# A four-layer graph network on one core: where VectorE's scoring work is put beside a pair's last layer

## The chip, the cores and the metric

One core of one Trainium2 chip runs the kernel. The metric is the device time of one execution in microseconds (us): the median of several runs. One further execution was taken with the profiler; every line of the profile comes from that one.

## The reference, cut to what matters

The input x has 64 graphs of 256 nodes with 256 features; all share one sparse 256 x 256 matrix adj. Four layers follow each other. Layers 0, 1 and 3 are the same function with other weights:

```python
pre_u = einsum('bud,dk->buk', h, W1[:d]);  pre_v = einsum('bvd,dk->bvk', h, W1[d:])
hidden = relu(pre_u[:, :, None, :] + pre_v[:, None, :, :] + b1)
S = sigmoid(hidden @ W2 + b2)                      # one score for each pair of nodes
a = einsum('buv,bud->bvd', S * adj, h);  m = einsum('uv,bud->bvd', adj, h) * h
z = beta1 * h + beta2 * (a @ Wa + ba) + beta3 * (m @ Wm + bm)
```

Layer 2 is an attention layer over the same graphs: one logit per node, softmax of leaky_relu(f_i + f_j) + adj, then a product with the features and a residual.

## The kernel before, in words

Only the pairs of nodes that adj joins (the edges) are scored. They are laid out once as tiles of 128 edges. For one scored layer of two graphs, a tile's sums pre_u + pre_v come in one of two ways. A **made** tile is a matmul on TensorE: `ga<-pre,pick`, from rows that ScalarE copied to `pre`. A **fetched** tile is two indirect DMAs that GpSimd (POOL) issues: the rows of a table of pre_u are gathered (`fetched<-tableu`), then those of pre_v are added to them (`fetched<-tablev`). The tables are written to DRAM by SyncE's queue (`tableu<-pu`, `tablev<-pv`). Either way VectorE (DVE) then scores the tile with one instruction for each of two graphs (`junk<-ga` or `junk<-fetched`), which leaves one column in `raw`. Most scored layers have eight made and eight fetched tiles, two groups (own, two nodes' diagonal) and one tile `left` with what remains.

The columns are rated twice in a scored layer, by `rated_all` (L740): ScalarE's tanh `val<-raw`, an add, and four multiplies `rm<-gva,val` on VectorE. EARLY needs the first four fetched tiles (numbered 0 to 3 here), the first four made ones, the diagonal and `left`. LATE needs the other tiles and comes last, from `end()` (L808). After it TensorE can `spread` (L865) the scores into the matrix `sa` (`ps<-rm,gu`), which the layer's `finish` (L368) multiplies with the graphs. `early(st)` (L849) starts `sa` from EARLY's scores (`ps<-ro,guo`, `sa<-diag,val,ps`).

Four graphs are worked on at a time: the first pair (side "a") and the second pair (side "b"). The function `beside` (L911) writes one **unit** of the program: the scores of one pair's layer (heavy), and the other pair's dense work of the neighbouring layers (light), which is a generator. After each piece of light work it yields a step (p, f): so many made tiles and so many steps of the fetched ones are traced there. A plain number is p alone. Six units make a round, and there are 16 rounds. They are called here after the pair and the layer that is scored: A0, B0, A1, B1, A3, B3. The light work of B3 is the first pair's `after` of the last layer, then its next graphs' `before` of layer 0. The light work of A0 is the second pair's last layer and its next graphs' layer 0. `halfway` (L900) interleaves these two: four steps of `after`, two of `before`, the rest of `after`, the rest of `before`.

Three lists give the steps: `STEPS` (L45) for `finish`, the local list `beside` in `before` (L656) for the four blocks of pre_u and pre_v, and a step (99, 99) after them that takes all that is left.

The program is traced in this order, and a planner then orders each engine's instructions: trace order is the priority, but an instruction that its reckoning finds ready sooner may be issued first. `tc.issue_after(x)` keeps an instruction behind x on x's engine. The flag `placed` decides whether the scores use it:

- `stay` (L706) keeps made matmuls, scores of fetched tiles, `left`, the diagonal and `val` behind the last instruction traced on their engine, so they stand mid-unit where the steps put them. Without `placed` the planner may move them.
- In `got` (L783), with `placed`, the fifth fetched step needs four made tiles, rates EARLY, and `early(st)` is a step of its own. Without it, all made tiles are traced first, then `left` and EARLY in one step, and `early(st)` comes after the sixth fetched tile.

The third value that `stream` (L885) yields with a unit's light work is that unit's `placed`. For the unit beside the last layer it is `i > 0`, on both sides.

POOL's fetches are one chain in trace order: `fetch` (L814) puts each behind the one before. Each unit's first six are issued as soon as its tables' first half is traced.

Of the kernel before, what the change touches and what calls it, by code (L numbers as in the profile page):

```python
# [17 lines left out]
GNN = ("L0_gnn_", "L1_gnn_", "L3_gnn_")  # L18
LAST = GNN[2]
# [25 lines left out]
STEPS = {  # L45
    GNN[0]: [(1, 1), (1, 1), (0, 1), (1, 0), (0, 1), (2, 1)],
    GNN[1]: [0, 0, 0, (0, 1), (0, 1), 1],
    LAST: [1, (1, 1), 0, (1, 1), (0, 1), (2, 1)],
}

VEC = {}
# [11 lines left out]
def blk(c):  # L63
    return slice(c * P, (c + 1) * P)
# [37 lines left out]
def adj_seq_kernel(ctx: ExitStack, tc: tile.TileContext, a: dict, out: bass.AP):  # L102
# [44 lines left out]
    def sca(name):  # L147
        return scas[:, SCA[name] : SCA[name] + 1]
# [141 lines left out]
    def stages(pools):  # L290
# [7 lines left out]
        def psum():  # L298
            return ps.tile([P, 2, 256], FP, tag="ps", name="ps")

        def product(o, lhs, rhs):

            for m in range(2):
                for c in range(2):
                    mm(out=o[:, m, :], lhsT=lhs[:, c, blk(m)], rhs=rhs[:, c, :], start=c == 0, stop=c == 1)
# [7 lines left out]
        def hT_tile(st):  # L313
            return one.tile([P, 2, 2, N], FP, tag="hT" + st["side"], name="hT")

        def h_tile(st, g):
            return fm.tile([P, 2, D], FP, tag=f"h{g}" + st["side"], name=f"h{g}")

        def of_graph(x, b):
            return x[bass.ds(b, 1)].rearrange("b (p c d) -> (b p) c d", p=P, c=2)  # L320
# [32 lines left out]
        def kept(st, l):  # L353

            hb = one.tile([P, 2, 2, N], FP, tag="hb", name="hb")
            for i in range(2):
                if l == LAST:
                    for m in range(2):
                        vector.scalar_tensor_tensor(
                            hb[:, i, m, :], st["h"][i][:, m, :], sca(l + "beta1"), zbrow, ALU.mult, ALU.add  # L360
                        )
                else:
                    scalar.activation(
                        hb[:, i], st["hT"][:, i], AF.Identity, bias=zbias[l][:, i : i + 1], scale=sca(l + "beta1")
                    )
            return hb

        def finish(st, l):  # L368

            sa, mT = st["sa"], st["mT"]  # L370
            hb = kept(st, l)
            aT = one.tile([P, 2, 2, N], FP, tag="aT", name="aT")
            for g in range(2):
                t = psum()
                product(t, st["h"][g], sa[:, :, g, :])
                scalar.copy(aT[:, :, g, :], t)
                yield STEPS[l][g]
            if l == LAST:
                for g in range(2):
                    z = psum()  # L380
                    for m in range(2):
                        for j, (w, y) in enumerate(((wm[l], mT), (wa[l], aT))):
                            for c in range(2):
                                mm(out=z[:, m, :], lhsT=y[:, c, g, blk(m)], rhs=w[:, c, :],
                                   start=j == 0 and c == 0, stop=j == 1 and c == 1)
                        yield STEPS[l][2 + 2 * g + m]
                    o = h_tile(st, g)
                    vector.tensor_tensor(o, hb[:, g], z, ALU.add)
                    nc.sync.dma_start(
                        out=of_graph(out, st["b"] + g), in_=o  # L390
                    )
                return
            hT = hT_tile(st)
            for m in range(2):
                z = psum()
                for j, (w, y) in enumerate(((wm[l], mT), (wa[l], aT))):
                    for c in range(2):
                        mm(out=z, lhsT=w[:, c, blk(m)], rhs=y[:, c], start=j == 0 and c == 0, stop=j == 1 and c == 1)
                    if j == 0:
                        yield STEPS[l][2 + 2 * m]  # L400
                vector.tensor_tensor(hT[:, m], hb[:, m], z, ALU.add)
                yield STEPS[l][3 + 2 * m]
            st["hT"] = hT
            st["h"] = []

            def turn(g):
                t = psum()
                flip(t, hT[:, :, g, :])
                h = h_tile(st, g)
                if l == GNN[1]:  # L410

                    vector.tensor_tensor(h, t, bias2.unsqueeze(1).to_broadcast([P, 2, D]), ALU.add)
                else:
                    scalar.copy(h, t)
                st["h"].append(h)

            if l == GNN[1]:
                for g in range(2):
                    turn(g)
                    yield 0  # L420
            else:

                st["turn"] = turn
# [78 lines left out]
    def few(stack):  # L502
# [143 lines left out]
        def before(st, l):  # L646

            hT = st["hT"]
            pu = one.tile([P, 2, 2, D], FP, tag="pu" + st["side"], name="pu")
            pv = one.tile([P, 2, 2, D], FP, tag="pv" + st["side"], name="pv")  # L650
            pre = one.tile([P, len(FAST), 2 * D], FP, tag="pre" + st["side"], name="pre")
            order = [(m, g) for m in range(2) for g in range(2)]
            if l == LAST:
                order = [(m, g) for g in range(2) for m in range(2)]

            beside = {LAST: [0, (0, 1), (0, 1), (0, 1)], GNN[1]: [0] + [(0, 1)] * 3, GNN[0]: [(0, 1)] * 4}[l]  # L656
            beside = dict(zip(order, beside))
            st["tables"] = [
                tables.tile([N, 2 * D], FP, tag="table" + t + st["side"], name="table" + t) for t in "uv"
            ]  # L660

            st["pu"], st["pv"], st["pre"] = pu, pv, pre
            if l != GNN[1]:
                st["own"] = one.tile([P, 2, 2, D], FP, tag="own", name="own")
            t = one.tile([P, FIRST, 2, D], FP, tag="fetched" + st["side"], name="fetched")
            st["fetched"] = [t[:, f] for f in range(FIRST)]
            for m, g in order:
                if l == LAST and (m, g) == (1, 0):
                    st["flip"](1)
                t = psum()  # L670
                for c in range(2):
                    mm(out=t, lhsT=hT[:, c, g, blk(m)], rhs=w1[l][:, c], start=c == 0, stop=c == 1)
                scalar.copy(pu[:, m, g, :], t[:, 0, :])
                vector.tensor_tensor(pv[:, m, g, :], t[:, 1, :], b1row[l], ALU.add)
                if g == 1:
                    for rows, x in zip(st["tables"], (pu, pv)):
                        nc.sync.dma_start(out=rows[blk(m)], in_=flat(x)[:, m])
                    if m == 0:
                        st["fetches"] = list(FETCHES_MORE if more(st, l) else FETCHES)

                        if numbered:
                            fetch(st, AHEAD)
                if l != GNN[1]:
                    vector.tensor_tensor(st["own"][:, m, g, :], t[:, 0, :], pv[:, m, g, :], ALU.add)
                if g == 1:
                    if m == 0:
                        rows_u(st, 0, 2, 0, 0)
                    rows_v(st, 4 - 4 * m, 2, 0)
                    st["rows"] = scalar.last.ins
                yield beside[(m, g)]  # L690
                if l == GNN[1] and (m, g) == (0, 1):
                    st["turn"](0)
                    yield 0, 1
                    st["turn"](1)
                    yield 0
            yield REST_OF_IT

            yield from mixed(st, l, later if past else None, (0,) if more(st, l) else (0, 1))
# [186 lines left out]
        def stream(side, starts):  # L885

            sts = [{"b": b, "side": side} for b in starts]
            load(sts[0])
            short = [before(sts[0], GNN[0])]
            for i, st in enumerate(sts):  # L890
                yield short, (st, GNN[0]), i > 0
                yield [after(st, GNN[0]), before(st, GNN[1])], (st, GNN[1]), True
                yield [after(st, GNN[1]), attention(st), before(st, GNN[2])], (st, GNN[2]), False
                short = [after(st, GNN[2])]
                if i + 1 < len(sts):
                    load(sts[i + 1])
                    short = [halfway(after(st, GNN[2]), 4, before(sts[i + 1], GNN[0]), 2)]
            yield short, None, False
# [149 lines left out]
```

## Time and profile before

| what | us |
|---|---|
| median of 5 runs | 3474.66 |
| lowest and highest of them | 3470.12 and 3475.57 |
| the profiled execution | 3478.15 |
| its span, first to last instruction | 3476.4 |
| TensorE (PE) busy | 3365.6 |
| VectorE (DVE) busy | 2650.0 |
| POOL busy | 2412.7 |
| ScalarE (ACT) busy | 1556.3 |
| mean granted TensorE clock | 0.989 |

The profiled execution took 1.75 us more than its span, and 3.5 us more than the median. The page lists engines, DMA queues, the chain of work that ended last, and groups of instructions. Nearly all instructions have line 79, a helper, so groups are told apart by their tiles: `out<-in`. In a timeline row the columns are start, length, engine, line, operation, tiles, shapes, count, and in brackets the engine's idle time before it with what ended it.

### The profile page before, as it was taken

To read this page: it belongs to the slowest core of one execution; us is meant where nothing else is said; L and a number is where in the kernel's file an instruction comes from. 1 tells how busy PE (TensorE), PEld (TensorE's weight loads), DVE (VectorE), ACT (ScalarE), POOL (GpSimd) and SP (SyncE) were. 2 spreads that over 40 slices of the span, in tenths; PEclk is the share of its full clock that TensorE was granted. 3 is DMA by queue.
4 is the path that set the end of the run, shared out by engine and by line. 5 is a ranking of instruction groups with operands and counts; after the bars stand their busy time and mean duration, and the time that the engine had idled before them with its cause. 6 is when DMAs were issued, how large, how long until landed. Compare 5 with 4: busy or idle time off the path is not lost.

```text
span 3476.4 us, 48323 instructions
## 1 busy us (share of the span) xinstructions
PE 3365.6 (97%) x14200; PEld 2074.6 (60%) x14200; DVE 2650.0 (76%) x10523; ACT 1556.3 (45%) x2833; POOL 2412.7 (69%) x1882
## 2 busy tenths in 40 slices
PE   6999999999999999999999999999999999999998
PEld 3566565665656556565665656656565665656655
DVE  4777787877877777777777878777787777777776
ACT  2444444444444444544444444444444444444442
POOL 3667777677676767677677776776767776777774
PEclk7999999999999999999999999999999999999999
DMA  5788787887878878788787888778788887888875
GB/s 147 159 180 189 168 197 171 191 180 172 198 168 195 171 179 191 175 187 181 176 191 167 196 173 189 179 168 202 165 190 181 178 191 171 193 184 175 191 164 121
DMA packets 289070, 620.81 MB, mean 179 GB/s; under 512 B 39072, under 2 KB 56352, under 8 KB 288800
## 3 DMA queue, kind: packets, MB, share of 16 engines
q0 software_dynamic: 204800, 461.49, 66.4%
q1 hardware_dynamic: 82416, 154.96, 12.7%
q8 instruction: 115, 1.88, 0.2%
q10 hardware_dynamic: 1584, 1.20, 0.1%
q14 instruction: 155, 1.27, 0.1%
HBM read 500.06 MB, written 117.44 MB: 178 GB/s over the span
## 4 chain that ended last, share of the span: by engine, by line
PE 71%; POOL 9%; DMA 8%; issue 6%; DVE 4%; ACT 2%; ACTq 0%; POOLq 0%; DVEq 0%
PE ps L79 55%; PE ga L79 16%; POOL fetched L827 8%; DMA fetched<-tablev,ids_v 4%; DVE junk L79 2%; DMA fetched<-tableu,ids_u 2%; DMA tableu<-pu 1%; POOL left L827 1%; ACT pre L79 1%; DVE sa L79 1%; DVE rm L79 0%; ACT val L79 0%; ACT pu L79 0%; DVE own L79 0%; DVE pv L79 0%
## 5 line engine op out<-in xcount | busy, mean ns | idle before, releaser
L827 POOL DMA_INDIRECT fetched<-tablev,ids_v x832 | 1316.5, 1582 | 385.5 <-issue 254.4
L827 POOL DMA_INDIRECT fetched<-tableu,ids_u x832 | 839.9, 1010 | 553.3 <-DMA tableu<-pu 292.1
L79 DVE SCALAR_TENSOR_TENSOR junk<-fetched,L_gnn_w2row 128x256 f32<-128x256 f32 x1664 | 641.2, 420 | 209.0 <-DMA fetched<-tablev,ids_v 205.2
L79 PE MATMUL ga<-pre,pick 128*128 128x512 f32 x1408 | 726.6, 610 | 27.5 <-ACT pre L79 16.0
L79 PE MATMUL ps<-L_gnn_w,hT 128*128 128x512 f32 x1536 | 708.6, 599 | 5.5 <-DMA hT<-in_xT_dram 5.5
L79 DVE SCALAR_TENSOR_TENSOR junk<-ga,L_gnn_w2row 128x256 f32<-128x256 f32 x1408 | 536.1, 419 | 94.7 <-PE ga L79 85.4
L79 PEld LDWEIGHTS ps<-L_gnn_w,hT 128*128 128x128 f32 x1536 | 280.4, 191 | 324.3 <-issue 297.8
L79 ACT COPY pre<-pv 64x512 f32<-64x512 f32 x704 | 434.1, 617 | 62.6 <-DVE pv L79 49.7
L79 PE MATMUL ps<-sa,h 128*128 128x256 f32 x1536 | 367.6, 384 | 19.9 <-DVE sa L79 14.0
L79 PEld LDWEIGHTS ps<-sa,h 128*128 128x128 f32 x1536 | 293.2, 192 | 137.1 <-issue 69.0
L79 ACT COPY pre<-pu 64x1024 f32<-64x1024 f32 x352 | 361.5, 1044 | 6.7
L79 ACT COPY pu<-ps 128x256 f32<-128x256 f32 x384 | 143.0, 372 | 472.3 <-PE ps L79 441.3
L79 PEld LDWEIGHTS ga<-pre,pick 128*128 128x128 f32 x1408 | 249.2, 191 | 171.4 <-issue 101.1
L79 DVE TENSOR_TENSOR rm<-gva,val 128x256 f32<-128x256 f32 x768 | 277.7, 420 | 60.5 <-ACT val L79 51.8
L79 PE MATMUL ps<-adj,h 128*128 128x256 f32 x1280 | 295.5, 382 | 3.7 <-issue 3.7
L79 PEld LDWEIGHTS ps<-adj,h 128*128 128x128 f32 x1280 | 245.3, 192 | 78.7 <-issue 43.2
L79 ACT ACTIVATE hb<-hT,L_gnn_zbias,scas 128x512 f32<-128x512 f32 x128 | 97.3, 806 | 414.5 <-DVE hT L79 366.7
L79 ACT COPY aT<-ps 128x512 f32<-128x512 f32 x192 | 112.5, 586 | 326.5 <-PE ps L79 300.7
L79 PEld LDWEIGHTS ps<-rm,gu 128*64 128x64 f32 x3072 | 179.7, 138 | 131.5 <-issue 76.5
L79 DVE TENSOR_TENSOR pv<-ps,L_gnn_b1row 128x256 f32<-128x256 f32 x384 | 161.9, 422 | 123.4 <-ACT pu L79 114.0
L79 PE MATMUL ps<-rm,gu 128*64 128x128 f32 x3072 | 220.2, 282 | 31.4 <-DVE rm L79 21.7
L79 PE MATMUL ps<-mT,L_gnn_Wm 128*128 128x512 f32 x512 | 240.6, 592 | 0.0
(149 smaller groups left out, 4212.1 us busy)
## 6 DMA issues: line engine op xcount, KB each, us to landing
tableu<-pu SPq DMA_DIRECT2D x192, 256.0 KB
tablev<-pv SPq DMA_DIRECT2D x192, 256.0 KB
hT<-in_xT_dram SPq DMA_DIRECT2D x32, 512.0 KB
h<-in_x_dram SPq DMA_DIRECT2D x64, 256.0 KB
out_dram<-h SPq DMA_DIRECT2D x64, 256.0 KB
fetched<-tableu,ids_u POOLq DMA_INDIRECT x832
fetched<-tablev,ids_v POOLq DMA_INDIRECT x832
L_gnn_w<-in_L_gnn_W_dram SPq DMA_DIRECT2D x6, 256.0 KB
```

Source lines behind the costliest of these rows:

```text
L79: self.last = getattr(self.engine, op)(*a, **k)
L827: this = nc.gpsimd.indirect_dma_start(out=to, out_offset=None, in_=rows, in_offset=bass.IndirectOffsetOnAxis(ap=ids, axis=0), compute_op=( ...
```

## The change

In `stream`, `placed` for the unit beside the last layer becomes `i > 0 and side == "b"`. So the scores of A0 (15 of 16 times) stay placed, and those of B3 no longer are. The last B3, beside which no new graphs are begun, was not placed before either.

The steps of the light work are told apart by side. Beside the first pair's last layer (unit B3) the steps of `finish` become 1, 1, (0, 1), (1, 1), (0, 1), (2, 1), and those of the following `before` 0, 0, (0, 2), (0, 1). Beside the second pair's (unit A0) they stay as they were but for the last of `finish`, (2, 2) where it was (2, 1): there the fifth fetched tile is traced one step sooner, and so are the sixth and the seventh, which follow it.

No instruction is added or removed; only their order can change.

```diff
 STEPS = {
     GNN[0]: [(1, 1), (1, 1), (0, 1), (1, 0), (0, 1), (2, 1)],
     GNN[1]: [0, 0, 0, (0, 1), (0, 1), 1],
-    LAST: [1, (1, 1), 0, (1, 1), (0, 1), (2, 1)],
+    LAST + "a": [1, 1, (0, 1), (1, 1), (0, 1), (2, 1)],
+    LAST + "b": [1, (1, 1), 0, (1, 1), (0, 1), (2, 2)],
 }
...
         def finish(st, l):
 
             sa, mT = st["sa"], st["mT"]
+            beside = STEPS[l + st["side"] if l == LAST else l]
...
-                yield STEPS[l][g]
+                yield beside[g]
...
-            beside = {LAST: [0, (0, 1), (0, 1), (0, 1)], GNN[1]: [0] + [(0, 1)] * 3, GNN[0]: [(0, 1)] * 4}[l]
+            beside = {LAST: [0, (0, 1), (0, 1), (0, 1)], GNN[1]: [0] + [(0, 1)] * 3, GNN[0]: [(0, 1)] * 4 if st["side"] == "b" else [0, 0, (0, 2), (0, 1)]}[l]
...
-                yield short, (st, GNN[0]), i > 0
+                yield short, (st, GNN[0]), i > 0 and side == "b"
```

More of the change, by code (lines that the diff above doesn't have):

```diff
@@ L385, in finish @@
                                    start=j == 0 and c == 0, stop=j == 1 and c == 1)
-                        yield STEPS[l][2 + 2 * g + m]
+                        yield beside[2 + 2 * g + m]
                     o = h_tile(st, g)
@@ L399, in finish @@
                     if j == 0:
-                        yield STEPS[l][2 + 2 * m]
+                        yield beside[2 + 2 * m]
                 vector.tensor_tensor(hT[:, m], hb[:, m], z, ALU.add)
-                yield STEPS[l][3 + 2 * m]
+                yield beside[3 + 2 * m]
             st["hT"] = hT
```

## The prediction

> **What bounds the kernel.** I read the page first, its parts 1 and 4.
>
> ```profile
> PE 3365.6 (97%) x14200; PEld 2074.6 (60%) x14200; DVE 2650.0 (76%) x10523; ACT 1556.3 (45%) x2833; POOL 2412.7 (69%) x1882
> ...
> PE 71%; POOL 9%; DMA 8%; issue 6%; DVE 4%; ACT 2%; ACTq 0%; POOLq 0%; DVEq 0%
> ```
>
> TensorE is busy 97% of the span, yet the chain that ended last runs through POOL and DMA for 17%. So a reordering can win only where TensorE waits, and there the question is who is last. I cut the span at the LATE ratings (ScalarE's `val<-raw` with 16 columns) and took busy times for one B3, A0 and B0 from the windows view. Its columns: stretch and length, then busy time and count of each engine.
>
> ```profile
> 1726.83:1762.19 35.36, 34.30 (x160) 22.28 (x158) 26.91 (x106) 14.37 (x25) 26.10 (x21) 1.00 0.86 213
> 1762.19:1793.48 31.29, 29.68 (x124) 19.75 (x120) 24.59 (x100) 14.77 (x25) 24.23 (x19) 1.00 0.85 194
> 1793.48:1824.50 31.02, 31.02 (x125) 17.51 (x124) 23.18 (x96) 15.78 (x28) 20.62 (x17) 1.00 0.79 162
> ```
>
> TensorE lacks 1.06 us in B3 and 1.61 in A0; VectorE (third engine) has 7 to 8 us free in each. Fourteen inner rounds, measured so from timeline rows, give a mean of 0.83 us lacking in B3, 1.12 in A0 and 0.06 in B0; their B3 last 34.8 us, their A0 31.6. Where A0's lack comes from stands at the end of B3, in the timeline:
>
> ```profile
> 1755.12 1.54 POOL L827 DMA_INDIRECT fetched<-tablev,ids_v  x1 [0.30 <-issue]
> ...
> 1761.32 1.09 PE L79 MATMUL ps<-rm,gu 128*64 128x128 f32 x16
> 1761.38 0.43 DVE L79 SCALAR_TENSOR_TENSOR junk<-fetched,L_gnn_w2row 128x256 f32<-128x256 f32 x1 [1.29 <-DMA fetched<-tablev,ids_v]
> ...
> 1762.19 0.31 ACT L79 ACTIVATE val<-raw,L_gnn_halfb 128x16 f32<-128x16 f32 x1 [2.66 <-DVE junk L79]
> ...
> 1764.03 1.33 PE L79 MATMUL ps<-rm,gu 128*64 128x128 f32 x16 [1.61 <-DVE rm L79]
> ```
>
> The eighth fetched tile's second DMA is issued at 1755.12, its score starts 6.26 us later, LATE follows, and TensorE stands 1.61 us before the second half of `spread`. VectorE had waited 1.29 us for that landing: here the fetch chain is last, not VectorE. In the 14 rounds VectorE waits over 0.5 us for this landing in nine, and at most 0.1 in five; the score starts 5.2 to 6.9 us after the issue.
>
> **Part one: A0's step (2, 2).** It moves the two scores of the fifth fetched tile ahead of the first pv and own of block 1, and the sixth and seventh tile one place each. VectorE at the end of A0:
>
> ```profile
> 1787.51 0.42 DVE L79 SCALAR_TENSOR_TENSOR junk<-ga,L_gnn_w2row 128x256 f32<-128x256 f32 x1
> ...
> 1788.78 0.42 DVE L79 TENSOR_TENSOR pv<-ps,L_gnn_b1row 128x256 f32<-128x256 f32 x1 [0.84 <-ACT pu L79]
> 1789.24 0.42 DVE L79 TENSOR_TENSOR own<-ps,pv 128x256 f32<-128x256 f32 x1
> 1789.58 0.42 DVE L79 SCALAR_TENSOR_TENSOR junk<-fetched,L_gnn_w2row 128x256 f32<-128x256 f32 x1
> ...
> 1793.02 0.42 DVE L79 SCALAR_TENSOR_TENSOR junk<-fetched,L_gnn_w2row 128x256 f32<-128x256 f32 x1
> ```
>
> Before the first pv VectorE idles 0.84 us. A fetched tile's two scores, one 0.34 us after the other, take 0.76 with the last read-out, so they fill this hole. Their data is there: the fifth tile's second DMA leaves at 1778.24, and 6.9 us later it is 1785.1. Everything behind comes 0.69 us sooner (two scores at their pitch), as far as landings allow: the eighth tile's DMA leaves 23.9 us into A0 on the mean, lands 5.2 to 6.9 later (29.1 to 30.8, say 29.9), and would be scored from 29.8 instead of 30.5. So LATE comes 0 to 0.69 sooner; I take 0.5.
>
> What that is worth shows in the `spread` that follows, against one that waits for nothing (at the start of B3). Rows of TensorE, B3 then A0's successor B0:
>
> ```profile
> 1729.14 1.97 PE L79 MATMUL ps<-rm,gu 128*64 128x128 f32 x32
> 1731.03 1.98 PE L79 MATMUL ga<-pre,pick 128*128 128x512 f32 x4
> ```
>
> ```profile
> 1794.29 2.35 PE L79 MATMUL ps<-rm,gu 128*64 128x128 f32 x32
> 1796.58 1.98 PE L79 MATMUL ga<-pre,pick 128*128 128x512 f32 x4
> ```
>
> From `spread` to the next made tile it is 1.89 us there and 2.29 here: 0.40 is waiting for LATE's `rm` and the `pre` copy behind `val`. This is the whole gain to be had, since after it TensorE has no work that could come sooner. Nearly the same wait stands in all 14 rounds. Bounds: 0 (every landing late) to 0.40 a round; I take **0.35**, near the upper row, since 0.5 sooner covers it in most rounds. B0 lies on the chain with TensorE alone, so it counts fully: 15 x 0.35 = 5.3 us. What the moved tiles delay: pv of block 1 starts at 88.69 or 88.78 either way, so the table writes on SyncE's queue and POOL's next fetches keep their time; no DMA is moved. If the hole were gone, pv, own, the table and `pre` would come 0.69 later, under the cover of 3.62 us of `ps<-adj,h` that TensorE has there.
>
> **Part two: B3 without placing.** No work goes; `stay` goes, and tiles 1 to 4, `left`, EARLY and `early` are traced later. Three things can move.
>
> POOL: the order of its chain is the same. Buffers that its fetches need are scored long before (A0's fifth fetch is issued 8 us after B3's last score). So the eighth tile lands when it did: cost 0.
>
> TensorE: inside B3, past its first 10 us, I find only changes of shape of 0.1 to 0.3 us, so nothing is to be won. Two made tiles and `ps<-ro,guo` change places among full work: cost 0.
>
> VectorE: it decides only through LATE. Against: four `hb` instructions of the next unit (two rows of 0.87, one at 1755.56) stand before the last tiles in B3; unplaced tiles, traced earlier, would go first, and where VectorE is last (five rounds in 14) LATE could come up to 1 us sooner. That is 5/14 x 15 x 1 = 5 us at most. For it: a free planner puts a fetched score where it reckons the data there, and VectorE then stands. Two places show that, an unplaced B1 and the last B3, which was never placed:
>
> ```profile
> 1655.89 0.43 DVE L79 SCALAR_TENSOR_TENSOR junk<-fetched,L_gnn_w2row 128x256 f32<-128x256 f32 x1 [2.76 <-DMA fetched<-tablev,ids_v]
> ```
>
> ```profile
> 3448.07 0.43 DVE L79 SCALAR_TENSOR_TENSOR junk<-fetched,L_gnn_w2row 128x256 f32<-128x256 f32 x1 [2.98 <-DMA fetched<-tablev,ids_v]
> ...
> 3448.76 1.43 DVE L79 TENSOR_TENSOR rm<-gva,val 128x256 f32<-128x256 f32 x4
> ```
>
> In the second, EARLY's `val` was done at 3445.7, but its four `rm` came only after a stall of 2.98 us and the scores. In an inner B3 what is queued behind such a stall is `rm`, h, made scores, pv, own and the last tiles; LATE waits for them. VectorE idles 0.95 us on the mean in the last 10 us before LATE, so a stall costs what exceeds that: up to 2.98 - 0.95 = 2.0 us a round. Bounds of part two are -5 us and 15 x 2.0 = +30 us. I take 0: nearest to the row at 1761.38, where the landing, which does not move, is last in nine rounds of 14.
>
> The Trainium skill speaks against part two: "TensorE: Matmul & The Clock Gate", section "Architectural detail", says that VectorE's queue is strictly first in, first out. The two stalls agree: scores of made tiles stood behind the one at 1655.89 and ran as soon as it had. By that rule alone a stall would cost its whole length, 15 x 2.98 = 45 us; with the idle time only the excess counts.
>
> The same page's section "What's actually happening" states that an idle window of about 3.4 us halves the clock. The windows above show a clock of 1.00 with holes of up to 1.6 us, and the longest at this place in 14 rounds is 3.0. A hole grown past that would by the page cost some 1.7 us more a round, an estimate that no row here shows and the sum leaves out.
>
> **Sum.** The profiled execution: 3478.15 - 5.3 + 0 = 3472.9. It lay 3.5 above the median; from 3474.66 the same step gives 3469.4, rounded **3470**.
>
> **Rivals.**
>
> *VectorE stalls in B3.* Unlanded scores ahead of `rm` and pv push LATE back. It decides once a stall exceeds the 0.95 us of idle time. With a stall of 2.2 us, between none and 2.98, LATE is 1.25 late: 15 x 1.25 = 18.8, less 5.3: about 3488; with the full 2.0, 3474.7 + 30 - 5.3 = 3499. For it: the two rows, and waits of 205 us in all for these landings, mostly in unplaced units. Against: in those units the end is still the landing of the last tile. Slower.
>
> *VectorE's end in B3 is relieved too.* `hb` leaves the last stretch, the five rounds gain: 3474.7 - 5.3 - 5 = 3464. Against: the landing is only a little sooner there.
>
> *The order hardly changes, or the eighth landing in A0 takes the gain.* With bounds of 0 on both parts it is 3474.7. For it: A0's eighth tile lands within 0.7 us of being needed.
>
> **How the numbers follow.** Forecast 3470: 0.37. Stalls: 0.29, over 3475 to 3499. Relieved: 0.20. No change: 0.14. A measurement of this kernel tells about 0.2%, 7 us, from no change: faster is below 3467.7, slower above 3481.6. Faster: the relieved case and 0.12 of the forecast's (both gains at their full size), 0.32. Slower: most of the stall case, 0.26. The rest, 0.42, lies within. The range is 3460 (a few us below the relieved case) to 3492 (above the middle of the stall case): it leaves out 0.1 above and less below. The likeliest case alone spans 3466 to 3475.
>
> **What would show it.** Right: in A0 a fetched tile's scores stand before the first pv of block 1, LATE comes 0.3 to 0.69 sooner, and from `spread` to the next made tile in B0 takes 1.9 to 2.0 instead of 2.29. In B3 the eighth score still starts 5.2 to 6.9 us after its DMA's issue, and the hole at the start of A0 stays as it was. Wrong: VectorE rows in B3 with over 1 us before a fetched score and `rm` or pv behind, B3 over 35.5 us on the mean, the hole in A0 grown; or B0 unchanged because A0's eighth tile is waited for.

## The result and the profile after

The changed kernel took 3479.62 us, the median of 34 runs (3471.98 to 3494.73), against 3473.00 for the kernel before on the same chips (57 runs): a ratio of 1.0023, 95% interval 1.0016 to 1.003. It is **slower by 6.6 us**. The forecast was 3470 and faster, so the sign was wrong; the time lies inside the range. The kernel before has medians from 3460.7 to 3473.0 us on the chips used here, so every comparison below is a ratio to the kernel before on the same chip.

The profiled execution took 3481.51 us, its span is 3479.8 and its granted clock 0.988. The page's busy times and shares of the chain for it:

```profile
PE 3363.4 (97%) x14200; PEld 2074.6 (60%) x14200; DVE 2651.4 (76%) x10523; ACT 1555.7 (45%) x2833; POOL 2412.8 (69%) x1882
...
PE 68%; POOL 10%; DMA 8%; issue 6%; DVE 5%; ACT 2%; another core or an unknown queue 0%; POOLq 0%; ACTq 0%; DVEq 0%; SPq 0%
```

Each engine is busy as long as before to within 2.2 us, so the loss lies in the order, in what waits for what. TensorE's share of the chain fell from 71 to 68%. B3 and the A0 behind it in the same round as before, from the windows view (stretch and length, then busy time and count of PE, PEld, DVE, ACT, POOL, granted clock, DMA share, GB/s):

```profile
1734.40:1770.09 35.69, 34.76 (x162) 22.79 (x161) 25.68 (x104) 14.38 (x25) 25.81 (x21) 1.00 0.88 214
1770.09:1801.17 31.08, 29.31 (x118) 19.54 (x119) 25.86 (x103) 14.76 (x26) 22.93 (x18) 1.00 0.79 177
```

B3 grew by 0.33 us and A0 shrank by 0.21. VectorE has 1.2 us less to do in B3 and 1.3 more in A0: of the four `hb`, which all stood ahead of B3's last scores, three now stand behind them. Means over the 14 inner rounds, cut at the LATE ratings, with a second profile of either kernel, both taken on another chip:

| us | before | before again | after | after again |
|---|---|---|---|---|
| length of B3 | 34.80 | 34.78 | 35.40 | 35.36 |
| length of A0 | 31.59 | 31.69 | 31.27 | 31.19 |
| length of B0 | 31.07 | 31.10 | 31.35 | 31.27 |
| TensorE's lag in A0's first 6 us | 2.18 | 2.14 | 3.19 | 2.94 |
| TensorE's lag in B0's first 6 us | 0.84 | 0.94 | 0.48 | 0.45 |
| eighth tile of B3: its score after its second DMA's issue, in rounds where VectorE waits over 0.3 us for it | 6.28 | 5.87 | 6.73 | 6.62 |

The lag is what the starts of TensorE's matmuls fall behind their usual spacing, so time at a lowered clock is in it; the choice of the usual spacing moves it by about 0.1 us. The idle time alone in A0's first 6 us is 1.12 and 1.10 us before, 1.50 and 1.41 after. The two rows on TensorE hold nearly the whole balance: it gains 0.36 to 0.49 us a round at the start of B0 and loses 0.8 to 1.0 at the start of A0. Fifteen times the difference, 0.3 to 0.65, is 5 to 10 us; measured were 6.6.

**The gain.** VectorE at the end of A0, from the timeline (start, length, engine, line, operation, tiles, in brackets the idle time before it):

```profile
1796.12 0.42 DVE L80 SCALAR_TENSOR_TENSOR junk<-fetched,L_gnn_w2row 128x256 f32<-128x256 f32 x1
...
1796.70 0.42 DVE L80 TENSOR_TENSOR pv<-ps,L_gnn_b1row 128x256 f32<-128x256 f32 x1
1797.16 0.42 DVE L80 TENSOR_TENSOR own<-ps,pv 128x256 f32<-128x256 f32 x1
...
1800.35 0.43 DVE L80 SCALAR_TENSOR_TENSOR junk<-fetched,L_gnn_w2row 128x256 f32<-128x256 f32 x1 [0.36 <-DMA fetched<-tablev,ids_v]
```

A fetched tile's scores now stand ahead of the first pv, and the idle 0.84 us before it is gone. In this round the eighth tile is already waited for, by 0.36 us. TensorE at the start of B0:

```profile
1802.22 2.17 PE L80 MATMUL ps<-rm,gu 128*64 128x128 f32 x32
1804.32 1.98 PE L80 MATMUL ga<-pre,pick 128*128 128x512 f32 x4
```

From `spread` to the next made tile it is 2.10 us in this round, and 1.90 in the median round, where it was 2.29.

**The loss.** The end of B3, TensorE, VectorE, POOL and SyncE's queue together:

```profile
1762.42 1.54 POOL L829 DMA_INDIRECT fetched<-tablev,ids_v  x1 [0.47 <-DMA fetched<-tableu,ids_u]
...
1763.34 1.14 PE L80 MATMUL ps<-ro,guo 64*128 64x256 f32 x8
...
1763.85 0.33 SPq L679 DMA_DIRECT2D tableu<-pu  x1
...
1765.20 0.33 SPq L679 DMA_DIRECT2D tablev<-pv  x1
...
1769.28 0.42 DVE L80 SCALAR_TENSOR_TENSOR junk<-fetched,L_gnn_w2row 128x256 f32<-128x256 f32 x1 [0.83 <-DMA fetched<-tablev,ids_v]
...
1770.09 0.31 ACT L80 ACTIVATE val<-raw,L_gnn_halfb 128x16 f32<-128x16 f32 x1 [3.63 <-DVE junk L80]
...
1771.86 1.42 PE L80 MATMUL ps<-rm,gu 128*64 128x128 f32 x16 [1.85 <-DVE rm L80]
```

In the kernel before, the two table writes in this stretch are:

```profile
1757.51 0.33 SPq L677 DMA_DIRECT2D tableu<-pu  x1
...
1758.27 0.33 SPq L677 DMA_DIRECT2D tablev<-pv  x1
```

and block 1's `ps<-L_gnn_w,hT`, whose results these writes carry, stands behind `ps<-ro,guo` there:

```profile
1751.45 1.14 PE L79 MATMUL ps<-ro,guo 64*128 64x256 f32 x8
...
1753.48 3.60 PE L79 MATMUL ps<-L_gnn_w,hT 128*128 128x512 f32 x8
```

In the changed kernel it stands ahead of the `ps<-ro,guo` at 1763.34:

```profile
1759.82 3.60 PE L80 MATMUL ps<-L_gnn_w,hT 128*128 128x512 f32 x8
```

Count from the issue of the eighth tile's second DMA, 1762.42 here and 1755.12 before. The writes of block 1's tables follow it by 1.43 and 2.78 us here, by 2.39 and 3.15 before. The score follows by 6.86 us, before by 6.26; TensorE then waits 1.85 us, before 1.61. Over 14 rounds the writes leave at 29.30 and 30.65 us into B3, before at 30.35 and 31.32. In the 6 us from the issue SyncE's queue starts packets of 413 KB on the mean of these rounds, before 296; in the second profiles it is 407 and 340. The next unit's first fetched tile tells the same: its second DMA, which waits for the first one's landing, is issued 6.15 us after the first instead of 5.77 (in the second profiles 5.93 and 5.78). So it is not the eighth tile alone whose transfer takes longer there.

What the longer wait sets off shows in another round, from the windows view of the changed kernel; 921 to 924 holds the wait at A0's start:

```profile
910.00:921.00 11.00, 10.85 (x52) 6.40 (x50) 9.98 (x44) 3.02 (x7) 7.53 (x6) 1.00 0.98 236
921.00:924.00 3.00, 1.14 (x15) 1.00 (x16) 3.00 (x12) 2.81 (x5) 2.37 (x2) 1.00 0.42 100
924.00:928.00 4.00, 4.00 (x10) 1.82 (x8) 3.50 (x13) 3.22 (x4) 3.09 (x4) 0.57 0.84 149
928.00:932.00 4.00, 4.00 (x18) 3.14 (x17) 2.94 (x14) 0.58 (x1) 3.39 (x3) 1.00 0.82 142
```

After TensorE stood about 2 us, its granted clock was 0.57 over the next 4 us and 1.00 again behind. Four made tiles take 3.65 us there instead of 1.98:

```profile
924.21 3.65 PE L80 MATMUL ga<-pre,pick 128*128 128x512 f32 x4
```

An A0 with such a stretch of half clock lasts 32.2 us in the changed kernel, one without 30.7: 1.5 us more.

### The profile page after: what moved, and what is told of

It is laid out like the page before. It is cut to its first block, busy times and chain, and to the rows that moved or that the text cites. A ratio compares the mean times of both kernels' runs of the same rounds, so it can differ in the third digit from the quotient of the medians.

```text
span 3479.8 us, 48338 instructions
## 1 busy us (share of the span) xinstructions
PE 3363.4 (97%) x14200; PEld 2074.6 (60%) x14200; DVE 2651.4 (76%) x10523; ACT 1555.7 (45%) x2833; POOL 2412.8 (69%) x1882
## 4 chain that ended last, share of the span: by engine, by line
PE 68%; POOL 10%; DMA 8%; issue 6%; DVE 5%; ACT 2%; another core or an unknown queue 0%; POOLq 0%; ACTq 0%; DVEq 0%; SPq 0%
PE ps L80 53%; PE ga L80 15%; POOL fetched L829 9%; DMA fetched<-tablev,ids_v 5%; DVE junk L80 2%; DMA fetched<-tableu,ids_u 1%; DMA tableu<-pu 1%; POOL left L829 1%; ACT pre L80 1%; DVE rm L80 1%; DVE sa L80 1%; ACT pu L80 0%; DVE mT L80 0%; DMA hT<-in_xT_dram 0%; ACT val L80 0%
## 5 line engine op out<-in xcount | busy, mean ns | idle before, releaser
L80 PE MATMUL ps<-aT,L_gnn_Wa 128*128 128x512 f32 x512 | 240.6, 592 | 0.0
```

Source lines behind the costliest of these rows:

```text
L80: self.last = getattr(self.engine, op)(*a, **k)
```

## Experiments

The theory at the start: part one gains what was forecast, and part two loses more because its table writes come beside the eighth landing. The rivals: VectorE stalls on scores put ahead of unlanded data; or VectorE's own order ends B3 later.

**Part one alone** (B3 as before):

```diff
-    LAST: [1, (1, 1), 0, (1, 1), (0, 1), (2, 1)],
+    LAST + "a": [1, (1, 1), 0, (1, 1), (0, 1), (2, 1)],
+    LAST + "b": [1, (1, 1), 0, (1, 1), (0, 1), (2, 2)],
```

> The kernel before with the step (2, 2) beside the second pair's last layer as its only edit; unit B3 stays placed with its old steps. My theory (the step in A0 gains, B3 without placing loses): 0.33 us less stall of TensorE at the start of B0 in each of 15 rounds, B3 unchanged at 34.8 us: 5 us faster than before, ratio 0.9985. Rival (the step in A0 itself is what costs): as slow as the full change, ratio 1.002 or more.

Measured: 0.9988 (0.9976 to 1.0), 3459.38 against 3463.14 us, a gain of 3.8, with an interval that reaches to nothing. The commonest A0 falls from 31.29 to 30.60 us. Its mean in this profile hardly does (31.54 us, in the two profiles of the kernel before, on other chips, 31.59 and 31.69): in five rounds of 14 the eighth tile of A0 is waited for (0.42 to 1.31 us), in five half clock follows the gap at A0's start, and these take part of the gain.

**Part two alone** (all of the change but A0's step):

```diff
+    LAST + "a": [1, 1, (0, 1), (1, 1), (0, 1), (2, 1)],
+    LAST + "b": [1, (1, 1), 0, (1, 1), (0, 1), (2, 1)],
...
-                yield short, (st, GNN[0]), i > 0
+                yield short, (st, GNN[0]), i > 0 and side == "b"
```

(and the `before` list of the change)

> The full change without the step (2, 2): B3 unplaced, with its new steps; A0 as before. My theory: B3 still takes 0.6 us more a round and nothing is given back at B0: 5 us slower than the full change, ratio to before 1.0037 (1.003 to 1.005). Rival (the step in A0 is what costs): as fast as before, ratio 1.000.

Measured: 1.0034 (1.0021 to 1.0047), 11.5 us lost. So the loss is all in part two. These two ran on one chip, and there VectorE waits over 0.3 us for the eighth landing of B3 in 13 rounds of 14 in both, so their landings compare without a choice of rounds: the writes leave at 28.34 and 29.69 us instead of 29.78 and 31.02, the score comes 6.44 us after the issue instead of 6.09, and TensorE's longest gap at A0's start grows from 1.92 to 2.25 us on the mean. SyncE's queue starts 452 KB in the 6 us from the issue, in part one alone 284. The profiled execution of part two is a quick one, 3464.71 us where the median is 3474.61, so its profile shows less than the loss.

**The flag alone** (`i > 0 and side == "b"`, all steps as before):

> The kernel before with only the flag changed: B3 unplaced, its old steps kept. If the freedom of the planner is what costs, B3 grows by 0.6 us as in the full change: ratio 1.003. If the later steps are what costs (scores and EARLY piled up at the unit's end), B3 keeps 34.8 us: ratio 1.000. The order of VectorE has the second and third fetched tile ahead of the first pv here, so a stall of 1 to 2 us there is expected by both, which TensorE need not feel.

Measured: 1.0039 (1.0024 to 1.0054). Here the rival of the prediction is real. VectorE in B3, from the timeline of this kernel:

```profile
1752.23 0.43 DVE L79 SCALAR_TENSOR_TENSOR junk<-fetched,L_gnn_w2row 128x256 f32<-128x256 f32 x1 [3.37 <-DMA fetched<-tablev,ids_v]
...
1752.58 1.43 DVE L79 TENSOR_TENSOR rm<-gva,val 128x256 f32<-128x256 f32 x4
```

VectorE stands 3.37 us before the sixth fetched tile, with `rm`, pv and own queued behind; 2.68 us on the mean of 14 rounds. B3 lasts 35.86 us.

**The steps alone** (B3's new steps, still placed, A0's step as before):

> The kernel before with only B3's new steps, still placed. If the later steps are what costs: eight scores of fetched tiles in a row stand at the end of B3, LATE comes at least 0.6 us later, ratio 1.003 or more. If the planner's freedom is what costs: ratio 1.000.

Measured: 1.0131 (1.0112 to 1.0151), the worst. TensorE in B3:

```profile
1768.65 1.20 PE L80 MATMUL ps<-ro,guo 64*128 64x256 f32 x8 [3.27 <-ACT ro L80]
```

With the scores held in trace order EARLY comes late, and `ps<-ro,guo` stands in TensorE's queue ahead of the last `ps<-L_gnn_w,hT`; TensorE idles 3.27 us before it on the mean of 14 rounds too. The flag and the steps each mend part of what the other breaks. In the whole change neither stall is left: no fetched score of B3 but the eighth is waited for by more than 0.14 us on the mean.

**Either kernel again,** unaltered:

> The kernel before, unchanged, for a second profile on the chip of the next three runs: ratio 1.000. B3 34.5 to 34.8 us, the eighth fetched tile of B3 scored 6.1 to 6.3 us after its second DMA's issue in the rounds where VectorE waits for it.

> The changed kernel, unchanged, for a second profile on the same chip: ratio 1.002. If the later landing is part of the cause, the eighth tile of B3 is scored 0.3 to 0.5 us later after its issue than in the kernel before (6.5 to 6.8 us), and LATE of B3 comes that much later; if that was chance of one profile, the two agree within 0.1 us.

Measured: 1.0001 (0.9983 to 1.0018) and 1.0017 (1.0 to 1.0033). Their profiles are in the table above and repeat the direction of its differences.

**Holding the writes.** Block 1's two table writes in B3 are kept in SyncE's queue behind a small DMA that reads LATE's columns of `raw`, so they leave when that unit's scores are in:

```diff
+                        if past and m == 1 and l == GNN[0] and st["side"] == "a":
+                            held.append((rows[blk(m)], flat(x)[:, m]))
+                        else:
                             nc.sync.dma_start(out=rows[blk(m)], in_=flat(x)[:, m])
...
             def end():
+                if held:
+                    mark = tables.tile([P, 16], FP, tag="mark", name="mark")
+                    first = nc.sync.dma_start(out=mark, in_=raw[:, LATE])
+                    with tc.issue_after(first.ins):
+                        while held:
+                            o, i = held.pop(0)
+                            nc.sync.dma_start(out=o, in_=i)
                 rated_all(LATE, 1)
```

On the changed kernel:

> The changed kernel with the two table writes of B3's block 1 (first pair, layer 0) held on SyncE's queue until B3's last scores: a small DMA that reads those scores is put ahead of them. The orders of VectorE and TensorE are those of the changed kernel. If the table writes, which come 1 us sooner in the changed kernel, delay the landing of B3's last tile: it is scored at most 5.9 us after its issue instead of 6.7, LATE comes 0.3 to 0.6 us sooner where VectorE waited for it, and ratio falls to 0.998 to 1.000, unless the later tables hold up POOL's fetches in A0. If VectorE's own order is the cause: landing and LATE as in the changed kernel, ratio 1.002 or more.

Measured: 0.9984 (0.997 to 0.9997), on the chip where the changed kernel alone has 1.0017. B3 lasts 34.68 us instead of 35.36. Its end, from the timeline:

```profile
1744.28 1.54 POOL L839 DMA_INDIRECT fetched<-tablev,ids_v  x1 [0.30 <-DMA fetched<-tableu,ids_u]
...
1750.38 0.42 DVE L80 SCALAR_TENSOR_TENSOR junk<-fetched,L_gnn_w2row 128x256 f32<-128x256 f32 x1
...
1751.18 0.33 SPq L815 DMA_DIRECT2D mark<-raw  x1
...
1751.60 0.41 SPq L819 DMA_DIRECT2D tableu<-pu  x1
...
1752.06 0.42 SPq L819 DMA_DIRECT2D tablev<-pv  x1
```

The writes leave after LATE's scores, and the eighth tile, issued at 1744.28, is scored 6.10 us later without a wait. VectorE waits over 0.3 us for it in 4 rounds of 14, where the changed kernel had 7 on this chip. The next unit's first fetched tile now has its second DMA 5.25 us after its first, where the changed kernel had 5.93 here, and SyncE's queue starts 39 KB in the 6 us from the eighth tile's issue instead of 407.

On part one alone, and on the kernel before:

> The kernel with the step (2, 2) alone, with the same two table writes held. By the landing theory the eighth tile of B3 is scored up to 0.8 us sooner and the hole of TensorE at the start of A0 (2.3 us of stall) shrinks by as much: ratio 0.995 to 0.998, the fastest so far, unless POOL's fetches in A0, which need these tables, come later. By the other theory 0.9988, as without the hold.

> The kernel before with held tables as the only edit. In the placed order the writes come 1 us later and meet the last landing less, so the hold is worth less than in the changed kernel, where it took off 0.0035: ratio 0.998 (0.9975 to 0.9990), 0.0012 above the kernel that has the step (2, 2) as well. If the hold is worth as much as there: 0.9965.

Measured: 0.997 (0.9954 to 0.9987), and 0.9985 (0.9969 to 1.0002). So holding seems to help the placed order too: about 0.0018 (against part one alone, on another chip) and 0.0015 there, 0.0033 in the changed one. The difference has the sign of the theory, but it is no larger than the intervals. And the changed B3 with held writes (34.68 us) is still longer than the placed one (34.32 and 34.07). So the writes are a cause of the changed kernel's time; that their earlier place is what part two lost is shown by the landings, not by these ratios, and by the length of B3 it is not all of it.

**`early` sooner.** On the changed kernel with held writes, `early(st)` is traced right after EARLY's rating in B3:

```diff
                         rated_all(EARLY, 0)
+                        if soon:
+                            early(st)
                         yield
```

> The changed kernel with held tables, and in B3 early(st) traced at once after EARLY's rating instead of two tiles later, so its matmuls stand between the two halves of the next graphs' pre_u and pre_v and its four sa instructions come before the last pv. If what is left of B3's loss (0.36 us of LATE against the placed order with held tables) is VectorE's work piled up at the unit's end, LATE falls towards 34.3 us and ratio from 0.998 to 0.997. If it is not the place of early, or if scores of tiles not yet landed take its place ahead of pv: 0.9985 or more.

Measured: 1.0003 (0.9986 to 1.0021), no gain. TensorE now idles 1.59 us on the mean in B3 before `ps<-ro,guo`, which stands ahead of the last `ps<-L_gnn_w,hT`. So the place of `early` is not shown to be the rest of the loss; the new wait may hide what it gained.

**Part one on both sides, with held writes:** `LAST + "a"` ends in (2, 2) as well.

> The best so far (placed on both sides, step (2, 2), held tables) with the step (2, 2) beside the first pair's last layer too. VectorE's order at the end of B3 then has the fifth tile before the first pv, as in A0. If VectorE is last in half of the rounds there, LATE of B3 falls by 0.2 to 0.5 us: ratio 0.994 to 0.996. If the landing of the eighth tile or a wait for the fifth takes its place: 0.997 or more.

Measured: 0.9968 (0.9949 to 0.9987). It beats both kernels, as part one with held writes does; between these two the intervals show no difference.

**Scores ahead of `h`.** In the changed kernel's B3 VectorE idles 9.6 us, before 7.8, and more of it stands before the two `h` of the first pair's last layer: 3.4 us between 15 and 25 us into the unit, before 1.3. Fetched scores whose rows had landed stand behind. So each `h` was put behind the fetched score traced last, and the first three fetched tiles were traced a step or two sooner (of the long line on `before` only the changed list is shown):

```diff
-    LAST + "a": [1, 1, (0, 1), (1, 1), (0, 1), (2, 1)],
+    LAST + "a": [1, 1, (0, 1), (1, 1), 0, (2, 1)],
...
-    ... [0, 0, (0, 2), (0, 1)]}[l]
+    ... [(0, 1), 0, (0, 2), (0, 1)]}[l]
...
-                    vector.tensor_tensor(o, hb[:, g], z, ALU.add)
+                    with tc.issue_after(scored.pop()) if scored and st["side"] == "a" else nullcontext():
+                        vector.tensor_tensor(o, hb[:, g], z, ALU.add)
```

> The changed kernel, with fetched scores of B3 kept ahead of the two h of the first pair's last layer: each h is issued behind the fetched score traced last, and the third fetched tile is traced one step sooner. Nothing is left out. Theory one, VectorE idles in front of h with ready scores queued behind: its idle time between 15 and 25 us into B3 falls from 4.7 us to 3.0 to 3.7, B3 from 35.4 to 34.4 to 34.9 us, and the time to 0.998 to 1.000 of the kernel before. Theory two, the loss comes from the table writes beside the eighth landing alone: the writes stay where they are in the changed kernel, B3 stays at 35.2 to 35.5 us, and the time at 1.0015 to 1.003. A loss against theory one would be an h that is late for what hangs on it: TensorE would stall at 20 to 30 us.

> The changed kernel unaltered, on the same chip as e10 and e12. Both theories: 1.0015 to 1.003 of the kernel before, B3 35.4 us.

> e10 with the two table writes of block 1 in B3 held until that unit's last scores are in. Nothing is left out. Theory one: holding takes some 0.7 us off a B3 in either order, so B3 is 33.7 to 34.2 us, and the time 0.995 to 0.997. Theory two: what the order costs was the writes, so it is as with held writes alone, 0.9984, B3 34.7 us.

Measured, on one chip: 0.9994 (0.9981 to 1.0007) with the scores ahead, 1.0031 (1.002 to 1.0042) for the changed kernel again, and **0.9953** (0.9935 to 0.997) with scores ahead and writes held, the fastest of all. The times are those of theory one, its mechanism is not: VectorE's idle time in B3 did not fall (10.0 us, in the changed kernel 9.2 on this chip), it only moved from before `h` to before made scores and the second fetched one, and B3 is as long in both profiles (35.06 and 35.00 us). What differs in the profiles is A0, 31.47 us against 32.23, with half clock in 6 rounds of 13 against 10, and how often the eighth landing is waited for over 0.3 us, 9 rounds against 13. The mean granted clock over all runs, 0.9891 against 0.9859, is by an estimate (0.001 is at most 3.5 us of this span) up to 11 of the 11.3 us between the two medians. Why the landing is waited for less often is open.

The same three profiles show the writes once more. With the writes as in the changed kernel the eighth score comes 6.58 and 6.54 us after its issue, with held writes 5.97; the next unit's first fetched tile has its second DMA 6.15 and 5.89 us after its first, with held writes 5.32. The kernel with the scores ahead and the one with the writes held as well differ in the hold alone, and the intervals of their ratios do not meet.

## Why the prediction was wrong

**What bounds the kernel** held: the same four steps, the landing, LATE, `rm`, the second half of `spread`, set the gap at A0's start after the change as well.

**Part one** was right in mechanism, and its size fits. LATE comes 0.67 us sooner in an undisturbed A0 (30.62 for 31.29; 0.5 was taken, 0.69 the bound). TensorE's lag at B0's start fell from 0.84 to 0.48 and from 0.94 to 0.45 us, where 0.35 was forecast. By itself it gave 3.8 us where 5.3 stood, though the interval there reaches to nothing; A0's eighth landing takes some of it, as the third rival said.

**Part two** failed at this step: "So the eighth tile lands when it did: cost 0." I had looked only at POOL's chain and at what its fetches wait for. The next unit's table writes on SyncE's queue lie in just that stretch, and with them nearer the tile's rows came later (6.44 us after the issue for 6.09 on one chip). The prediction traced the writes for part one ("no DMA is moved") and not for part two. There TensorE's order decides when they leave, and "Two made tiles and `ps<-ro,guo` change places among full work: cost 0" overlooked that block 1's `ps<-L_gnn_w,hT` moves ahead of `ps<-ro,guo`. The eighth tile leaves 0.2 us sooner and its score comes about 0.4 later after that: 0.35 on the one chip where all rounds but one can be compared, 0.45 and 0.75 by the waited rounds of the table.

**The clock** was named and left out of the sum, for want of a row. The profile before has such rows: two of its A0s have a stretch of half clock, the first from 1129 us on, after a gap of 2.06 us between starts, and they last 32.9 us on the mean where the others last 31.4.

```profile
1128.83 3.67 PE L79 MATMUL ga<-pre,pick 128*128 128x512 f32 x4
```

The Trainium skill, "TensorE: Matmul & The Clock Gate", section "What's actually happening", has the clock halved after at least one idle window of about 3.4 us. The runs disagree on the gap that it takes, and the measurement decides. Over 16 profiles, by the longest gap between starts of TensorE's instructions in the `spread` at A0's start: gaps under 1.5 us were followed by half clock in 0 of 97 rounds, 1.5 to 2.0 in 2 of 51, 2.0 to 2.5 in 14 of 28, 2.5 to 3.0 in 12 of 17, longer ones in 12 of 15. The changed order moved the mean gap from 1.68 and 1.50 to 2.04 and 2.03 us, to the edge of that step. Of 13 A0s, 2 and 2 had half clock before, 4 and 5 after, and 10 in the changed kernel's third profile; with held writes 0 or 1 in all six kernels. At 1.5 us each, 2.5 more in 13 is 0.29 us a round, or 4.3 us in 15 rounds, about as much as part one gains.

Counts from one profile are weak: part one alone, with B3 as before, had 5 of 13 on its chip. Every run of the experiments lists its mean granted clock, and that is the better measure. For the changed kernel it is 0.9885 against 0.9897 for the kernel before on one chip and 0.9859 against 0.9890 on another; for part two alone 0.9868 against 0.9885, for part one alone 0.9884 against 0.9885. As 0.001 of the clock is at most 3.5 us of this span, the lower clock is worth up to 4 and 11 us in the changed kernel and 6 in part two, by this estimate, where their medians lost 5.9, 9.0 and 11.5. With the writes held the clock is not below that of the kernel before in any of the six. So the lower clock can be half of what part two alone lost, and on the second of these chips all of what the changed kernel lost.

**VectorE** was put at 0 between -5 and +30, and the stall that I feared did not come in the whole change. It came with the flag alone, at 2.68 us on the mean, where 2.98 was the bound; the new steps take it away. What B3 loses besides the landing may be on VectorE's side: in the first profiles the rounds where VectorE waits for the landing are as long as they were (35.26 us before, 35.20 after) and those where it does not are longer (35.1 to 37.9, before 33.4 to 34.4). The second profiles do not repeat it: there the first kind grew too, from 34.96 to 35.67 us, and the second overlaps (34.1 to 36.0, before 33.7 to 36.6). So this is not shown, and neither is a cause: the place of `early` and the idle time before `h` were tried, and neither mechanism held. In ratios, part two costs 0.0034 as it is; with held writes on both sides it is 0.9984 against 0.997, so 0.0014 is left, with intervals that overlap.

**The sum** then reads, per round: 0.36 to 0.49 us gained at B0's start, as forecast, and 0.8 to 1.0 lost at A0's start, where 0 was forecast. By these profiles 0.3 to 0.4 us of that is idle time and about 0.3 half clock; the rest hangs on how the end of a matmul is counted. The eighth tile's transfer and the writes beside it are shown to be part of why the gap grew; whether they are all of it stays open.

## What to carry to other kernels

When instructions of one engine are reordered, follow every DMA that hangs on any engine's order in that stretch, writes too, and ask which transfer on the path to the end is then in flight beside them. Where the last wait of a stage is a landing, holding writes that nobody needs yet until it is in can be worth more than the reordering: 0.0015 (within the noise) to 0.0041 of the time here, and in four of six variants the kernel with it beat the kernel before clear of noise. Look at how close TensorE's gaps are to the length at which the granted clock drops in the profile's own windows; a few tenths more there can cost several times as much.

## What the runs showed of the hardware

- Gaps of 2 to 3 us between starts on TensorE were followed by 3.4 us of granted clock 0.5 (now and then 6.8) in 26 of 45 rounds, and gaps under 1.5 us in none of 97; an A0 with it was about 1.5 us longer in the kernels before and after.
- The two table writes, issued 0.5 to 1.3 us nearer to an indirect DMA's issue, went with 0.35 to 0.75 us more from its issue to the use of its rows, and held back, in the last three kernels, with 0.6 us less. Why, the runs do not show; the DMA engines were 79 to 90% busy in these units.
- Chips differ in more than speed. On some, the second `sa<-sa,ps` of a B3 started 1 to 4 us after the recorded end of the `ps<-rm,gu` matmul that it waits for, in 4 to 9 of 14 rounds (in the kernel before a matmul started at 1730.83 us and took 0.27; its signal came at 1733.70). TensorE idled 0.4 to 0.7 us a round 6 to 9 us into B3 there. On the chip of the first four experiments and on that of the last three neither occurred. The cause is open; it is in both kernels.
